# Graph layer with gathered and sorted edge groups: seven sorted pairs at every eleventh group in place of ten at every eighth

## Chip, cores and metric

The kernel runs on one core of a Trainium2 chip. The metric is the device time of one launch in microseconds (us). The engines are named as the profile names them: PE (TensorE), PEld (its weight loads), DVE (VectorE), ACT (ScalarE), POOL (GpSimd) and SP (SyncE).

## What is computed

One layer of a graph network on 6250 nodes of 128 features, with 100,000 edges that are sorted by destination, each with four attributes:

```
msg_in = concat([x[src], x[dst], edge_attr])          # 100000 x 260
h = silu(msg_in @ mW1 + mb1)                          # 100000 x 128
aggregated = segment_sum(h @ mW2 + mb2, dst, 6250)
u = silu(concat([x, aggregated]) @ uW1 + ub1)
y = layer_norm(x + u @ uW2 + ub2, ln_g, ln_b)
out = layernorm(x + y)
```

The kernel multiplies the node features by the two halves of mW1 first (tables A for sources and B for destinations), so that an edge needs the sum of a row of A, a row of B and four attributes times a small matrix. It sums the silu values by destination with a one-hot product and applies mW2 to the sums.

## The kernel before, in words

**Groups.** The edges are cut into 98 groups of 1024 (8 tiles of 128; the last has fewer). A group's destinations lie in a window of at most 80 nodes. The groups are worked off in one of two ways.

A **listed** group gets its rows of A by indirect DMA: POOL issues one gather for each tile (`fetch`, L272, `ga<-tab_a,src_i`), eight for a group, four listed groups ahead (`AHEAD`), into six buffers. DVE makes a matrix st of destinations (L670) and a one-hot matrix oh (L680). PE forms B's rows and the attributes' part (`pre<-mv,st`, eight products of one kind, 16 matmul records), DVE adds the gathered rows to it (L722, two halves), ACT takes silu (L724, two halves), and PE sums by destination (`pt<-oh,h`). One listed group is one **stage** of the program's main loop (`for j, g in enumerate(listed)`), and the hidden values of a group are made in the stage before its sums.

A **sorted** group gets no gathers. Sorted groups come in pairs k, k + 1. At the start of the program the edges of these groups are sorted by source (a bitonic sort on DVE, four rows of it for each group). With sorted sources, the rows of A are selected on PE: one-hot matrices O are multiplied by A, which lies in the core's memory in three bf16 pieces (`po<-O,A` for two of them, `po<-O,A_low` for the third); a window of the edges is enough for each block of nodes. A pair is worked off in four **parts** of 512 edges. For each part SP loads sources and destinations (`load_part`, L1089 to L1095, `sc<-sd` and `ar<-sd`), DVE makes st_s (L1114) and Oc, ACT makes most of O (squares at L1138 and relu at L1139, `picks`), PE multiplies the attributes (`pn<-Oc,at_s`, `attribute_part`) and adds B's rows (`po<-st_s,mv_s`), then comes the selection (`select`), ACT takes silu of the finished part (hT, L1198), PE turns it (`pn<-ident,hT`, `turned_hidden`), ACT copies it (h_s, L1209), and PE sums by destination (`pn<-oh,h_s`).

**The order of the work** is written out by hand. `Q0`, `QD` and `QN` give the first sorted group, the distance from pair to pair and the number of sorted groups. `SPAN` is QD - 2: the selection of a pair is spread over the listed stages between it and the pair before. Each stage has two slots for selections, one ahead of its sums and one behind (`slot(j, 0)` and `slot(j, 1)`). `shares` says how much of a pair's four parts each slot takes. `load_at`, `match_at`, `pick_at`, `part_at` and `turn_at` say for each of the four parts how many stages ahead of the pair its loads, its DVE matrices, its one-hot matrices O, its attribute products and its turning come; `ROWS` and `ATTR` say the same for the pair's rows of B and its attributes.

The gathers are paced. Every second gather waits for a product of PE (`paced`, at the end of the loop): the one that PE has reached 3.5 stages (`PACE`) ahead of the gather's own, counted in PE's work between pairs:

```
t -= (PACE if g < NG - 2 else PACE - 1) + NEAR * max(0.0, 1 - (t - RAW - 1) / (2 * RAW))
...
until = begun[knots[k]] + share * (begun[knots[k + 1]] - begun[knots[k]])
```

The nodes are worked off in batches of 512 beside the groups: tables A and B before, and the layer's second half after the last group of a batch (`node_stage`: u, uT, y, z and o, with PE products into pn).

Of the kernel before, what the change touches and what calls it, by code (L numbers as in the profile page):

```python
# [27 lines left out]
def kernel(  # L28
# [54 lines left out]
    last = [G * k + G for k in range(NB - 2)] + [NG - 4, NG - 1]  # L83
    assert rest_t == 5 and last[NB - 3] == NG - 10

    Q0, QD, QN = 18, 8, 20
    firsts = [Q0 + QD * q for q in range(QN // 2)]
    by_sort = {k + u: 2 * q + u for q, k in enumerate(firsts) for u in range(2)}
    listed = [g for g in range(NG) if g not in by_sort]
# [7 lines left out]
    HB = GE // 2  # L97
    QB = GE // GR
    SPAN = QD - 2
    shares = (0.3, 0.3, 0.4, 0.25, 0.375, 0.375, 0.35, 0.3, 0.35, 0.35, 0.35, 0.3)  # L100
    assert len(shares) == 2 * SPAN and abs(sum(shares) - GR) < 1e-6
    load_at, match_at, pick_at = (9, 8, 6, 5), (8, 7, 5, 4), (8, 6, 5, 3)
    part_at, turn_at = (7, 6, 4, 3), (4, 3, 1, 0)
    ROWS, ATTR = 7, 8
    SLACK = 400.0
    LISTS = 4
    assert RS <= P and W <= S0 and S0 + G * ED == P and listed[RAW] == RAW
# [1551 lines left out]
```

## Time and profile before

| | us |
|---|---|
| median of three runs | 1002.12 (1001.17 to 1003.69) |
| the profiled execution | 1000.51 |
| its span, from first to last instruction | 998.6 |
| PE busy | 781.4 |
| DVE busy | 609.6 |
| POOL busy | 590.1 |
| ACT busy | 456.7 |

The mean granted clock of PE was 0.910. In a row of a timeline the first number is the start in the span, the second the duration, and the square bracket holds the idle time of the engine before it and what ended that ("issue" is time in which it waited for nothing that the profile shows). In a row of the windows stand the stretch, its length, the busy time of each engine with its count of instructions, the granted clock, the share of the DMA engines and GB/s. In a row of waits stand the total, the number of times and the longest.

### The profile page before, as it was taken

Reading aid. Unit: us, or ns where it says so; the run is one execution under the profiler, and the core shown is the slowest. Engines: PE = TensorE matmul, PEld = TensorE weight load, DVE = VectorE, ACT = ScalarE, POOL = GpSimd, SP = SyncE. Lnnn points to the kernel's source line nnn. Section 1 sums busy time; section 2 is a strip of 40 time slices with the busy share of each in tenths; the row PEclk is TensorE's granted clock in tenths of the full one; section 3 lists DMA queues with packets and bytes.
Section 4 is the critical chain, followed back from the end, with each engine's and each line's share of the span. In section 5 each row is a group of like instructions: output and inputs, shape, how many; then the busy total and the mean of one; then the engine's idle time right before and its main releaser. Section 6 shows DMA issues by size and latency. Waiting matters only on the chain.

```text
span 998.6 us, 17635 instructions
## 1 busy us (share of the span) xinstructions
PE 781.4 (78%) x6000; PEld 680.4 (68%) x6000; DVE 609.6 (61%) x1631; ACT 456.7 (46%) x710; POOL 590.1 (59%) x633
## 2 busy tenths in 40 slices
PE   4547666787987998888887887988887987887844
PEld 3547665676776777777777766776676776776633
DVE  5457686875566566556566566576476475474562
ACT  4453021555356356356445545455455555542252
POOL 6666666566666656656666666666666666665630
PEclk8669887998999998999999999999899898997976
DMA  8554344533434434425334324334334334232220
GB/s 232 156 144 133 95 121 104 133 101 91 118 79 119 117 77 118 114 76 129 88 80 130 85 80 132 77 87 126 82 84 125 86 77 133 77 94 60 81 63 16
DMA packets 115619, 102.85 MB, mean 103 GB/s; under 512 B 24374, under 2 KB 95878, under 8 KB 115522
## 3 DMA queue, kind: packets, MB, share of 16 engines
q1 hardware_dynamic: 83430, 54.87, 19.3%
q0 software_dynamic: 19904, 40.80, 16.9%
q10 hardware_dynamic: 12188, 5.98, 2.1%
q8 instruction: 49, 0.80, 0.3%
q14 instruction: 48, 0.39, 0.1%
HBM read 87.26 MB, written 14.32 MB: 102 GB/s over the span
## 4 chain that ended last, share of the span: by engine, by line
PE 70%; issue 16%; DVE 5%; ACT 3%; DMA 2%; another core or an unknown queue 1%; SPq 1%; POOL 0%; DVEq 0%; ACTq 0%; POOLq 0%
PE po L167 24%; PE pre L167 15%; PE pt L167 14%; PE pn L167 13%; PE pn L170 2%; PE pre L170 1%; DVE keys L973 1%; DMA near<-near_d 1%; SPq L1074 1%; ACT A L528 0%; POOL ga L272 0%; DVE bn L792 0%; ACT xT L500 0%; DVE st L670 0%
## 5 line engine op out<-in xcount | busy, mean ns | idle before, releaser
L272 POOL DMA_INDIRECT ga<-tab_a,src_i x582 | 550.3, 946 | 350.6 <-issue 155.5
L167 PE MATMUL po<-O,A 128*128 128x314 bf16 (+54 forms) x1400 | 202.6, 251 | 18.2 <-issue 18.2
L167 PE MATMUL pre<-mv,st 128*128 128x128 f32 x1244 | 176.5, 288 | 33.4 <-issue 29.7
L167 PE MATMUL pt<-oh,h 128*128 128x104 f32 x1244 | 176.8, 293 | 30.6 <-issue 27.1
L167 PEld LDWEIGHTS pre<-mv,st 128*128 128x128 f32 x1244 | 161.2, 201 | 51.7 <-issue 46.9
L167 PEld LDWEIGHTS pt<-oh,h 128*128 128x128 f32 x1244 | 164.1, 208 | 38.9 <-issue 38.3
L167 PE MATMUL po<-O,A_low 128*128 128x314 bf16 (+54 forms) x700 | 161.0, 252 | 16.8 <-issue 16.7
L167 PEld LDWEIGHTS <-A 128*128 128x128 bf16 x1400 | 124.1, 102 | 43.1 <-issue 24.2
L724 ACT ACTIVATE h<-ga 128x512 f32<-128x512 f32 x146 | 86.2, 624 | 123.6 <-DVE ga L722 58.9
L722 DVE TENSOR_TENSOR ga<-ga,pre 128x512 f32<-128x512 f32 x146 | 94.5, 677 | 39.9 <-remote 10.5
L1198 ACT ACTIVATE hT<-po 128x512 f32<-128x512 f32 x40 | 23.9, 597 | 197.7 <-remote 96.9
L670 DVE TENSOR_SCALAR_CACHE_REDUCE st<-near,p_rows 80x1024 f32<-80x1024 f16 x78 | 98.7, 1265 | 13.1 <-issue 7.8
L1138 ACT ACTIVATE O<-sc,p_less 128x512 bf16<-128x512 f16 x160 | 105.5, 707 | 0.0
L779 DVE TENSOR_TENSOR acc<-acc,pt 128x80 f32 x78 | 18.5, 237 | 136.0 <-remote 46.8
L1139 ACT ACTIVATE O<-O,ones 128x1024 bf16<-128x1024 bf16 x80 | 91.8, 1148 | 2.6
L167 PEld LDWEIGHTS <-A_low 128*128 128x128 bf16 x700 | 69.6, 100 | 25.3 <-issue 16.8
L334 DVE TENSOR_TENSOR O<-sc,held 128x512 bf16<-128x512 f16 x160 | 57.4, 415 | 34.4 <-remote 26.9
L680 DVE TENSOR_TENSOR oh<-held,rel 128x640 f32<-128x640 f32 x78 | 63.5, 814 | 0.1
L1209 ACT COPY h_s<-pn 128x512 f32<-128x512 f32 x40 | 23.3, 581 | 83.4 <-remote 28.4
L167 PE MATMUL po<-st_s,mv_s 128*128 128x256 f32 x160 | 49.5, 438 | 8.3 <-ACT hT L1198 4.4
L272 POOL DMA_INDIRECT ga<-in_x_dram,src_i x40 | 38.1, 952 | 23.9 <-issue 11.0
L167 PE MATMUL pn<-Oc,at_s 128*128 128x256 f32 x160 | 45.2, 408 | 3.3 <-issue 1.8
(232 smaller groups left out, 905.0 us busy)
## 6 DMA issues: line engine op xcount, KB each, us to landing
near<-near_d SPq DMA_DIRECT2D x78, 160.0 KB
sc<-sd SPq DMA_DIRECT2D x80, 128.0 KB
ga<-tab_a,src_i POOLq DMA_INDIRECT x582
ar<-sd SPq DMA_DIRECT2D x40, 80.0 KB
mv<-tab_b SPq DMA_DIRECT2D x78, 40.0 KB
tab_b<-o SPq DMA_DIRECT2D x11, 256.0 KB
out_dram<-o ACTq DMA_DIRECT2D x11, 256.0 KB
x<-in_x_dram SPq DMA_DIRECT2D x10, 256.0 KB
```

Of the source, the lines that this page charges most:

```text
L167: counted(nc.tensor.matmul(to, *operands, **flags), to, share)
L170: counted(nc.tensor.transpose(to, *operands), to)
L272: ins = nc.gpsimd.indirect_dma_start(out=rows[g][:, i, :], out_offset=None, in_=x if g < RAW else tab_a[:, :], in_offset=bass.IndirectOffs ...
L334: nc.vector.tensor_tensor(cut(to), cut(of), few[:p, None, :].to_broadcast([p, n // FEW, FEW]), op=OP.is_equal)
L670: nc.vector.tensor_scalar(stbuf[turn_of(g) % NST][:W], near.pop(g), p_col[:W], 0.0, op0=OP.is_equal, op1=OP.add, accum_out=deg_col(g),)
L680: nc.vector.tensor_tensor(oh[g][:, :n, :W], w_row[:, None, :].to_broadcast([P, n, W]), rel[:, g, :n, None].to_broadcast([P, n, W]), op=OP. ...
L722: nc.vector.tensor_add(s[:, i], s[:, i], of)
L724: nc.scalar.activation(h[:, i], of, AF.Silu)
L1138: nc.scalar.activation(O[:, j], key, AF.Square, bias=p_less[:, r : r + 1])
L1139: nc.scalar.activation(O[:, 2:], O[:, 2:], AF.Relu, bias=ones[:, 0:1], scale=-1.0)
L1198: nc.scalar.activation(now["hT", u], now.pop(("po", u)), AF.Silu)
L1209: nc.scalar.copy(now["h"][:, :, 2 * u : 2 * u + 2, :].rearrange("p g i f -> p g (i f)"), px.rearrange("p (g i) f -> p g (i f)", g=2),)
```

## The change

Only numbers change, at three places of the head of the function:

```diff
-    Q0, QD, QN = 18, 8, 20
+    Q0, QD, QN = 21, 11, 14
...
-    shares = (0.3, 0.3, 0.4, 0.25, 0.375, 0.375, 0.35, 0.3, 0.35, 0.35, 0.35, 0.3)
+    shares = (0.2,) * 5 + (0.25,) * 4 + (0.2,) * 5 + (0.25,) * 4
...
-    load_at, match_at, pick_at = (9, 8, 6, 5), (8, 7, 5, 4), (8, 6, 5, 3)
-    part_at, turn_at = (7, 6, 4, 3), (4, 3, 1, 0)
-    ROWS, ATTR = 7, 8
+    load_at, match_at, pick_at = (12, 10, 8, 5), (11, 9, 7, 4), (11, 8, 6, 4)
+    part_at, turn_at = (10, 8, 6, 3), (6, 4, 2, 0)
+    ROWS, ATTR = 10, 11
```

The pairs now begin at groups 21, 32, 43, 54, 65, 76 and 87 in place of 18, 26 and so on to 90. There are 14 sorted groups in place of 20, and 84 listed groups, that is stages, in place of 78. `SPAN` becomes 9 in place of 6, so a pair's selection is spread over 18 slots in place of 12. Selections begin in stage 11 in both versions; they end in stage 70 before and in stage 73 now. Of SP's 688 instructions 659 are left.

On POOL the whole difference is this, at the start of the program and over its length (`pos_i` belongs to the sort, whose arrays have four rows for each sorted group; `ga` are the gathered rows):

```order
 L284 IOTA floor_i 1x96
 L287 IOTA ceil_i 1x112
-L291 IOTA pos_i 80x256
+L291 IOTA pos_i 56x256
 L272 DMA ga<-in_x_dram,src_i 128x128 x32
-L272 DMA ga<-tab_a,src_i 128x128 x582
+L272 DMA ga<-tab_a,src_i 128x128 x630
```

There are 48 gathers more, and the arrays of the sort are narrower.

On PE, before, at the head of the stage of a pair, where the last part of this pair is turned and the selection of the next pair's first part begins (a number behind a name is that of a buffer; `pre` is the next listed group's, `po` the bank of the selection):

```order
L167 MATMUL po<-O,A_low 128x2x72
L167 MATMUL pn<-w_87,xB 128x128 x4
L167 MATMUL pre<-mv_236,st_250 128x128 x8
L170 MATMUL pn<-ident,hT 128x128 x4
L167 MATMUL pn<-Oc,at_s_1370 128x256
L167 MATMUL pn<-Oc,at_s_1371 128x256
L167 MATMUL po<-st_s_1366,mv_s_1368 128x256
L167 MATMUL po<-st_s_1366,mv_s_1369 128x256
L167 LDWEIGHTS A
L167 MATMUL po<-O,A 128x2x51
```

Now, on PE at the head of the same stage:

```order
L167 MATMUL po<-O,A_low 128x2x72
L167 MATMUL pre<-mv_235,st_250 128x128 x8
L170 MATMUL pn<-ident,hT 128x128 x4
L167 MATMUL po<-st_s_1369,mv_s_1371 128x256
L167 MATMUL po<-st_s_1369,mv_s_1372 128x256
L167 LDWEIGHTS A
L167 MATMUL po<-O,A 128x2x51
```

The attribute products of the next pair's second part (`pn<-Oc,at_s`) no longer stand between the turning and the next selection; they come a stage later (8 stages ahead of their pair, with 9 stages between pairs).

On ACT, before, between the silu of a finished part (`hT`) and the copy of its turned values (`h_s`), in the middle of the program:

```order
L1198 ACTIVATE hT<-po 128x512
L724 ACTIVATE h_89<-ga 128x512 x2
L1138 ACTIVATE O<-sc,p_less 128x512 x2
L1139 ACTIVATE O<-O,ones 128x1024
L1138 ACTIVATE O<-sc,p_less 128x512 x2
L1139 ACTIVATE O<-O,ones 128x1024
L1209 COPY h_s<-pn 128x2x256
```

Now, on ACT between the two:

```order
L1198 ACTIVATE hT<-po 128x512
L724 ACTIVATE h_88<-ga 128x512 x2
L1209 COPY h_s<-pn 128x2x256
L724 ACTIVATE h_89<-ga 128x512 x2
L1138 ACTIVATE O<-sc,p_less 128x512 x2
L1139 ACTIVATE O<-O,ones 128x1024
```

The making of O has moved from between the silu and the copy to behind the copy.

## The prediction

> **What bounds the kernel now.** I read the page first, engine shares and chain, to see whether one engine is full.
>
> ```profile
> PE 781.4 (78%) x6000; PEld 680.4 (68%) x6000; DVE 609.6 (61%) x1631; ACT 456.7 (46%) x710; POOL 590.1 (59%) x633
> ...
> PE 70%; issue 16%; DVE 5%; ACT 3%; DMA 2%; another core or an unknown queue 1%; SPq 1%; POOL 0%; DVEq 0%; ACTq 0%; POOLq 0%
> PE po L167 24%; PE pre L167 15%; PE pt L167 14%; PE pn L167 13%; PE pn L170 2%; PE pre L170 1%; DVE keys L973 1%; DMA near<-near_d 1%; SPq L1074 1%; ACT A L528 0%; POOL ga L272 0%; DVE bn L792 0%; ACT xT L500 0%; DVE st L670 0%
> ...
> L272 POOL DMA_INDIRECT ga<-tab_a,src_i x582 | 550.3, 946 | 350.6 <-issue 155.5
> ```
>
> The chain runs through PE, its largest part the selections into po. POOL looks idle for 41%, but its busy time counts only the 946 ns of a gather, not what lies between two. The timeline of POOL shows that.
>
> ```profile
> 929.65 0.94 POOL L272 DMA_INDIRECT ga<-tab_a,src_i  x1 [1.86 <-issue]
> 930.90 0.94 POOL L272 DMA_INDIRECT ga<-tab_a,src_i  x1 [0.30 <-issue]
> ...
> 938.39 0.94 POOL L272 DMA_INDIRECT ga<-tab_a,src_i  x1 [0.30 <-issue]
> 943.17 0.94 POOL L272 DMA_INDIRECT ga<-tab_a,src_i  x1 [3.83 <-issue]
> ```
>
> Eight gathers start back to back from 929.65 to 938.39, so a gather costs POOL (938.39 - 929.65) / 7 = 1.249 us, and a listed group at least 8 x 1.249 = **9.99 us**. Between such runs it stops, here for 1.86 and 3.83 us.
>
> Next, how long a stage takes. Each listed group ends in one row of sums, so the rows of this kind in PE's timeline count the stages (the first listed group is stage 0).
>
> ```profile
> 193.03 1.93 PE L167 MATMUL pt<-oh,h 128*128 128x104 f32 x16
> ...
> 924.17 1.93 PE L167 MATMUL pt<-oh,h 128*128 128x104 f32 x16
> ...
> 984.06 1.56 PE L167 MATMUL pt<-oh,h 128*128 128x104 f32 x12 [0.42 <-DVE acc L779]
> ```
>
> These are stages 11, 71 and 77. Selections begin in stage 11 and end in stage 70, so 60 stages with selections took 924.17 - 193.03 = 731.1 us, 12.19 us each; six of them, with one pair, make a period of 73.1 us. The six stages after that took 10.0 us each, and 998.6 - 984.06 = 14.5 us follow. Three windows of about a period show what fills it.
>
> ```profile
> 489.00:562.00 73.00, 61.37 (x499) 54.02 (x499) 45.08 (x119) 36.95 (x56) 44.81 (x49) 0.95 0.37 97
> ...
> 635.00:708.00 73.00, 62.67 (x504) 52.45 (x503) 44.48 (x118) 38.16 (x57) 44.10 (x47) 0.98 0.36 95
> sum 219.00, PE 184.45 PEld 158.62 DVE 134.41 ACT 113.23 POOL 133.96; mean PE 61.48 PEld 52.87 DVE 44.80 ACT 37.74 POOL 44.65
> ```
>
> PE works 61.5 of 73 us. POOL's 48 gathers cost 48 x 1.249 = 60.0 us. Both are at 82 to 84%: neither is full, each waits for the other a little. POOL's waits say how: every second gather waits for a product of PE.
>
> ```profile
> POOL ga L272 <- issue: 166.6, 462, 5.2
> POOL ga L272 <- remote: 71.8, 48, 2.1
> POOL ga L272 <- PE po L167: 41.5, 33, 1.9
> ```
>
> That POOL follows PE, and is not merely slow, shows in the lead: the last gather of stage 37 started at 473.36, its sums at 508.6; the very last at 964.36, with its sums at 984.06, 19.7 us later. POOL can fall back by some 15 us before PE waits for rows.
>
> ```profile
> 473.36 0.95 POOL L272 DMA_INDIRECT ga<-tab_a,src_i  x1 [0.31 <-issue]
> ...
> 964.36 0.94 POOL L272 DMA_INDIRECT ga<-tab_a,src_i  x1 [0.30 <-issue]
> ```
>
> **The change part by part.** *Three pairs fewer.* Six groups go back from selection to gathers: 582 + 6 x 8 = 630 gathers. PE by tile, in the same three windows (po; Oc; hT; h_s; pre; oh, which holds h_s too; pn, which holds Oc, hT and h_s too):
>
> ```profile
> sum 219.00, PE 75.44; mean PE 25.15
> ...
> sum 219.00, PE 13.54; mean PE 4.51
> ...
> sum 219.00, PE 8.00; mean PE 2.67
> ...
> sum 219.00, PE 11.80; mean PE 3.94
> ...
> sum 219.00, PE 37.72; mean PE 12.57
> ...
> sum 219.00, PE 49.60; mean PE 16.53
> ...
> sum 219.00, PE 45.93; mean PE 15.31
> ```
>
> A pair costs PE 25.15 + 4.51 + 2.67 + 3.94 = 36.3 us; a listed group (12.57 + 16.53 - 3.94) / 6 = 4.19 us. So the change takes 3 x 36.3 - 6 x 4.19 = 84 us of work from PE and lays 48 x 1.249 = 60 us on POOL. What that is worth depends on which of the two ends last.
>
> *The new period* is nine stages and one pair. PE: 61.5 + 3 x 4.19 + 1.6 for three eighths more node work (15.31 - 4.51 - 2.67 - 3.94 = 4.2 us in a period) = 75.7 us, 8.4 us a stage. Its stalls are 73.1 - 61.5 = 11.6 us now; if they grow with the gathers (0.24 us each, 72 of them) they become 17.4 and the stage 10.3 us; if they keep their share of PE's work, 14.3 and 10.0 us. POOL: 72 x 1.249 = 89.9 us, 9.99 us a stage. So PE and POOL come out level and **POOL is late next**. I take 10.2 us, between the POOL floor and PE's upper value: PE has fewer stalls to give than before, as the gathers no longer wait for it.
>
> *The sum.* Stages 0 to 11 stay (193.0). Selections then run without a break from stage 11 to stage 73, so 63 stages (12 to 74) at 10.2 = 642.6. Nine stages without selection, 75 to 83, at the 10.0 of before = 90. The end is 14.5. Together 940.1, against a span of 998.6. The profiled run took 1000.51 as a whole, 1.9 more than its span, and the median of the runs is 1002.12; with the 1.9 the forecast is **942 us**. A stage of 11.13 us would give back exactly the old span: (998.6 - 297.5) / 63.
>
> *Eighteen smaller parts.* Each half-stage slot now holds 0.20 to 0.25 of a part in place of 0.25 to 0.40. The count of matmuls of a pair stays, so this costs nothing by itself; it spreads 25.15 us of po over nine stages, 2.8 us in each in place of 4.2. Less selection stands between a group's pre and its sums, and that was cover for DVE and ACT:
>
> ```profile
> L722 DVE TENSOR_TENSOR ga<-ga,pre 128x512 f32<-128x512 f32 x146 | 94.5, 677 | 39.9 <-remote 10.5
> ...
> L724 ACT ACTIVATE h<-ga 128x512 f32<-128x512 f32 x146 | 86.2, 624 | 123.6 <-DVE ga L722 58.9 <-issue 34.5 <-DMA ga<-tab_a,src_i 13.8
> L1138 ACT ACTIVATE O<-sc,p_less 128x512 bf16<-128x512 f16 x160 | 105.5, 707 | 0.0
> L1139 ACT ACTIVATE O<-O,ones 128x1024 bf16<-128x1024 bf16 x80 | 91.8, 1148 | 2.6
> L1198 ACT ACTIVATE hT<-po 128x512 f32<-128x512 f32 x40 | 23.9, 597 | 197.7 <-remote 96.9 <-PE pre L167 43.9 <-PE po L167 30.5
> L1209 ACT COPY h_s<-pn 128x512 f32<-128x512 f32 x40 | 23.3, 581 | 83.4 <-remote 28.4 <-PE po L167 22.7 <-PE pn L167 10.2
> ```
>
> The hidden values of a group are made a stage before its sums, so the add and the silu (2 x 677 + 2 x 624 ns) have a whole stage of about 10 us. I cost it at 0; without that cover it would be 2.6 us a stage.
>
> *Re-timed loads and matrices.* A part's DMAs on SP, its one-hot on ACT and its attribute products now come up to three stages further ahead of the pair. SP has 29 rows fewer in all. Between hT and h_s, ACT had two pairs of O squares (2 x (2 x 707 + 1148) = 5.1 us) and now often has one silu pair (1.25 us), so it stands at h_s waiting for PE's transposes; behind it stands the silu of the next listed group, which isn't due for a stage. Even if all of ACT's work grew with the listed groups, it would have 37.7 x 9 / 6 = 57 of 92 us, and DVE 44.8 x 9 / 6 = 67 of 92, so neither becomes the bound. What PE itself waits for hT is a row of its waits:
>
> ```profile
> PE po L167 <- ACT hT L1198: 4.4, 4, 2.0
> ```
>
> Cost 0; the upper end is a wait of 2.0 us, the longest of these, in each of 28 parts, 56 us; the lower end the 4.4 us that would go.
>
> *The start.* The sort works on 56 rows of partitions in place of 80, with as many instructions of the same length along a row, and two steps of node work change places. I put it at 0, and between -3 and +3 us.
>
> **The rivals.** *(a) The pace stays (slower).* POOL is gated at every second gather; in the stretch with selections it ran at 60.0 of 73.1 us, 82%, the rest being stops like those of 1.86 and 3.83 us. If the stops are a price of each run and not PE's slowness, the stage goes on taking 12.19 us, 63 of them 768, and the time is 297.5 + 768 + 1.9 = 1067 us. It decides from 1.39 us per gather (11.13 / 8). For it: a stop of 3.83 us follows just the run of eight, the longest. Against it: the wait is on PE's products by the program, PE will reach them sooner, and at 929.65 POOL went eight without a stop.
>
> *(b) The clock (same to slower).* PE's granted clock is lower where PE is less busy:
>
> ```profile
> 132.00:193.00 61.00, 43.34 (x278) 38.87 (x278) 49.65 (x134) 15.21 (x24) 36.68 (x40) 0.85 0.45 115
> ...
> 924.20:984.10 59.90, 40.21 (x243) 33.59 (x241) 31.15 (x94) 20.39 (x35) 23.63 (x25) 0.83 0.22 60
> ```
>
> It was 0.85 and 0.83 there, at 71 and 67% busy, against 0.95 to 0.98 at 84%. If the 10.2 us stage of a PE that is busy for 82% sank to 0.84, its 75.7 us would become 75.7 x 0.97 / 0.84 = 87.4, with 17.4 of stalls 104.8, 11.6 us a stage, 297.5 + 731 + 1.9 = 1030 us; half the fall gives 11.0 us and 992. Against it: 82% is far nearer to the 84% of the warm windows. The Trainium skill, "TensorE: Matmul & The Clock Gate", HAM oscillation, says that the clock is halved when PE idles for more than about 3.4 us and that a kernel whose products wait for DMA pays at every step; if each of the 63 stages held one such wait and 3.4 us at half rate behind it, 1.7 us would be lost in each, a stage would take 11.9 us and the run 1049 (an estimate from that page). The trace agrees that such waits are rare so far, the longest ones being:
>
> ```profile
> PE po L167 <- issue: 38.8, 62, 3.2
> PE pre L167 <- issue: 31.5, 43, 3.9
> ```
>
> *(c) The lead is spent (faster still).* If POOL runs without any stop from stage 11's end, its 550 gathers that are left then take 687 us; with 19.7 and 14.5 after the last this gives 193 + 687 + 34.2 + 1.9 = 916 us.
>
> *(d)* The change not doing what it says: the order of the instructions shows 630 gathers and 28 parts, so I leave this out.
>
> **How the numbers follow.** Forecast (stage 10.0 to 10.7, 928 to 974): 0.43. (c): 0.12. (b): 0.18, of it 0.05 faster, 0.05 same, 0.08 slower. (a): 0.27. So faster 0.60, same 0.05, slower 0.35, where 0.3% is about what a measurement of this kernel can tell. The range reaches from (c), 916, up to 1050: it leaves out half of (a) and half of (c). Where the forecast holds, its own range is 928 to 974.
>
> **What would show it.** Right: stages of about 10.2 us between stages 11 and 74; POOL's gathers at 1.25 to 1.3 us each in runs much longer than four, with 39 in 50 us in place of 33; PE at 74 to 77% of the span; the chain with POOL or gathers in it. Wrong: as many stops as before and 33 gathers in 50 us (a); a granted clock under 0.9 in the middle (b); a lead that has fallen under 20 us by the middle (c). If hT or st_s stand ahead of long waits of PE, the smaller cover was the cause, which I cost at nothing.

## The result and the profile after

The changed kernel takes 1061.32 us (median of 4 runs, 1059.25 to 1064.07) where the kernel before takes 1001.64 (1000.47 to 1003.69): the ratio is 1.0595, with a 95% interval of 1.0564 to 1.0626. It is slower by 60 us; the forecast was 942.

The page of the changed kernel, with the rows that answer to those of before (shares, granted clock by slice, chain, gathers, and PE's products of a listed group):

```profile
span 1060.1 us, 16188 instructions
...
PE 785.6 (74%) x5322; PEld 679.5 (64%) x5322; DVE 581.6 (55%) x1532; ACT 397.2 (37%) x626; POOL 635.9 (60%) x681
...
PEclk8769786888988897898888888988888888877876
...
PE 57%; issue 17%; DVE 10%; another core or an unknown queue 7%; ACT 5%; DMA 2%; DVEq 1%; POOL 1%; SPq 1%; ACTq 0%; POOLq 0%
...
L272 POOL DMA_INDIRECT ga<-tab_a,src_i x630 | 595.9, 946 | 366.5 <-issue 204.8
L167 PE MATMUL pre<-mv,st 128*128 128x128 f32 x1340 | 222.4, 321 | 43.0 <-issue 29.5
```

PE has far fewer products and is busy for 4 us more than before: one product pre takes 321 ns in place of 288, at a mean granted clock of 0.825 in place of 0.910. Everything else has less to do. Only POOL has more, and its idle time has hardly changed (366.5 us in place of 350.6).

The sums of stages 74 and 83 in PE's timeline, which stand for 924.17 and 984.06 of before (stage 11 ends at 191.8, within 1.3 us of before):

```profile
956.73 1.48 PE L167 MATMUL pt<-oh,h 128*128 128x104 f32 x12
...
1045.76 1.45 PE L167 MATMUL pt<-oh,h 128*128 128x104 f32 x11 [0.42 <-DVE acc L779]
```

The 63 stages took (956.7 - 191.8) / 63 = 12.14 us each. Before it was 12.19. By the costs of the prediction a stage has 18% less work for PE (8.4 us for 10.25), and it takes the same time, as rival (a) had it. The nine stages without selection took 9.9 us each and the end 14.3 us, as forecast. The windows show gathers at the pace of before:

```profile
300.00:350.00 50.00, 39.49 (x288) 34.30 (x287) 26.00 (x59) 18.41 (x28) 30.58 (x33) 0.86 0.34 92
700.00:750.00 50.00, 40.06 (x278) 35.57 (x277) 22.57 (x48) 14.95 (x25) 31.43 (x34) 0.83 0.35 95
950.00:1000.00 50.00, 37.70 (x241) 33.37 (x242) 26.48 (x66) 14.14 (x24) 32.73 (x35) 0.81 0.28 80
```

Still 33 to 35 gathers in 50 us, in the stretch with selections and in the one without. How this looks close up, on POOL and PE of the changed kernel at the same time:

```profile
851.49 0.94 POOL L272 DMA_INDIRECT ga<-tab_a,src_i  x1 [2.33 <-ACT h L724]
...
860.28 0.94 POOL L272 DMA_INDIRECT ga<-tab_a,src_i  x1 [0.30 <-issue]
863.76 0.94 POOL L272 DMA_INDIRECT ga<-tab_a,src_i  x1 [2.53 <-issue]
```

```profile
858.64 0.33 PE L167 MATMUL pt<-oh,h 128*128 128x104 f32 x1 [0.45 <-issue]
860.04 0.25 PE L167 MATMUL pt<-oh,h 128*128 128x104 f32 x1 [1.07 <-issue]
861.47 0.33 PE L167 MATMUL pt<-oh,h 128*128 128x104 f32 x1 [1.18 <-issue]
862.89 1.42 PE L167 MATMUL pt<-oh,h 128*128 128x104 f32 x6 [1.10 <-issue]
```

Late in a run of eight gathers PE issues one product in 1.4 us, products that take 0.25 to 0.33 us and wait for nothing that the profile shows; 1.7 us after the run's last gather has ended (861.2) it goes on at full pace, and 0.9 us after that so does POOL.

The kernel before itself takes 819 to 825 us in some of the jobs on the chip and 997 to 1005 us in others, the first measurement among them, so each run is compared with the kernel before of its own job, and I call the jobs quick and slow by that.

### The profile page after: what moved, and what is told of

The parts are those of the page before. It is cut to its first block, busy times and chain, and to the rows that moved or that the text cites. A ratio compares the mean times of both kernels' runs of the same rounds, so it can differ in the third digit from the quotient of the medians.

```text
span 1060.1 us, 16188 instructions
## 1 busy us (share of the span) xinstructions
PE 785.6 (74%) x5322; PEld 679.5 (64%) x5322; DVE 581.6 (55%) x1532; ACT 397.2 (37%) x626; POOL 635.9 (60%) x681
## 4 chain that ended last, share of the span: by engine, by line
PE 57%; issue 17%; DVE 10%; another core or an unknown queue 7%; ACT 5%; DMA 2%; DVEq 1%; POOL 1%; SPq 1%; ACTq 0%; POOLq 0%
PE pre L167 16%; PE po L167 15%; PE pt L167 12%; PE pn L167 11%; PE pn L170 2%; ACT O L1138 1%; DVE ga L722 1%; ACT O L1139 1%; DVE keys L973 1%; PE pre L170 1%; DVE oh L680 1%; DVE bn L792 1%; DVE st L670 1%; POOL ga L272 1%
## 5 line engine op out<-in xcount | busy, mean ns | idle before, releaser
L272 POOL DMA_INDIRECT ga<-tab_a,src_i x630 | 595.9, 946 | 366.5 <-issue 204.8
L167 PE MATMUL pre<-mv,st 128*128 128x128 f32 x1340 | 222.4, 321 | 43.0 <-issue 29.5
L167 PEld LDWEIGHTS pre<-mv,st 128*128 128x128 f32 x1340 | 204.8, 233 | 57.4 <-issue 41.9
L167 PE MATMUL po<-O,A 128*128 128x114 bf16 (+32 forms) x980 | 162.2, 267 | 25.9 <-issue 25.8
L167 PE MATMUL po<-O,A_low 128*128 128x114 bf16 (+32 forms) x490 | 122.3, 267 | 14.0 <-issue 14.0
L167 PEld LDWEIGHTS <-A 128*128 128x128 bf16 x980 | 94.4, 108 | 53.8 <-issue 37.6
L1138 ACT ACTIVATE O<-sc,p_less 128x512 bf16<-128x512 f16 x112 | 73.8, 706 | 0.0
L1139 ACT ACTIVATE O<-O,ones 128x1024 bf16<-128x1024 bf16 x56 | 64.3, 1148 | 1.8
L167 PEld LDWEIGHTS po<-st_s,mv_s 128*128 128x128 f32 x112 | 26.4, 262 | 51.4 <-ACT hT L1198 27.6
L334 DVE TENSOR_TENSOR O<-sc,held 128x512 bf16<-128x512 f16 x112 | 39.5, 414 | 0.2
```

What stands on the lines that cost most here:

```text
L167: counted(nc.tensor.matmul(to, *operands, **flags), to, share)
L272: ins = nc.gpsimd.indirect_dma_start(out=rows[g][:, i, :], out_offset=None, in_=x if g < RAW else tab_a[:, :], in_offset=bass.IndirectOffs ...
L334: nc.vector.tensor_tensor(cut(to), cut(of), few[:p, None, :].to_broadcast([p, n // FEW, FEW]), op=OP.is_equal)
L1138: nc.scalar.activation(O[:, j], key, AF.Square, bias=p_less[:, r : r + 1])
L1139: nc.scalar.activation(O[:, 2:], O[:, 2:], AF.Relu, bias=ones[:, 0:1], scale=-1.0)
```

## The experiments

Theories: **G**, POOL's gathers set the time, each costing a fixed time. **C**, PE sets it, slowed by its clock. **P**, the wait of every second gather for PE's products, seen late, sets it.

The first run without the pacing, the one with pre twice, the first without selection and the first with half of the gathers were priced from 1061 us and met quick jobs. Their times lie outside every range that was expected for them; they are read against 882.13 us, which the changed kernel took in another quick job.

**The pacing left out** (changed kernel).

```diff
-        tc.add_manual_dep(ins.ins, product_at[...].ins.name, ...)
+        pass
```

> The changed kernel without the pacing: gathers wait only for their buffers and queue. Theory P (the wait for PE's products, seen late, holds POOL at 1.48 us per gather): gathers then go at 1.25 us, runs far longer than eight, 39 in 50 us, the time falls to 930 to 980 us. Theory G (a gather costs POOL or its queue about 1.48 us with the stop behind its run, whoever waits): still 33 to 34 in 50 us, 1050 to 1070 us. Theory C (PE, slowed by its clock and by the gathers, sets the time): gathers go faster at first and then wait for buffers, the time stays within 2%, 1040 to 1080 us.

872.91 us, in a quick job (before 821.58). 662 gathers ran without one stop (never more than 0.32 us idle between two).

> The changed kernel without the pacing, once more. On a chip where before takes about 821 us: 870 to 876 us as before. On a chip where before takes about 1001 us: if the late wait on PE's products makes POOL's stops there (theory P), gathers at 1.25 us and 870 to 960 us; if the gathers stop by themselves (theory G with 1.48 us each), 1045 to 1065 us.

This one fell into a slow job (before 1005.12): 1261.52 us, a ratio of 1.257 (1.240 to 1.274), far outside of both expectations. The first 50 us of the two runs of this one kernel, quick job and slow job:

```profile
0.00:50.00 50.00, 28.04 (x183) 24.33 (x183) 31.44 (x87) 30.34 (x57) 36.22 (x47) 0.91 0.88 250
```

```profile
0.00:50.00 50.00, 8.59 (x45) 7.07 (x45) 11.55 (x40) 8.32 (x15) 35.98 (x47) 0.67 0.54 144
```

POOL does the same in both, 47 instructions, most of them gathers back to back. In the quick job PE has 183 matmuls beside them, in the slow one 45. After the last of the gathers from x POOL then stands still for 37 us:

```profile
53.83 0.94 POOL L272 DMA_INDIRECT ga<-in_x_dram,src_i  x1 [0.30 <-issue]
92.19 0.94 POOL L272 DMA_INDIRECT ga<-tab_a,src_i  x1 [37.41 <-DMA st<-ea_d]
...
POOL ga L272 <- ACT h L724: 315.7, 53, 16.9
```

The gather at 92.19 is the first from table A. The 40 gathers from x have filled five of the six buffers, so it can't be a buffer that it waits for; the last write of table A, which PE's products have to make first, starts at 89.5 us (47.4 in the quick job). Over the whole run POOL waits 315.7 us, 53 times, for the silu of a group whose buffer it needs. So in a slow job PE falls behind beside gathers back to back, and POOL then waits for what PE hasn't made or used. The pacing isn't what costs the time there; as I read it, it keeps the runs short. P falls.

**PE with more work** (changed kernel, every product pre issued twice).

```diff
+            if not raw:
+                matmul(to, st[:, i, :], mv[turn_of(g) % NM], start=True, stop=True)
             matmul(to, st[:, i, :], mv[turn_of(g) % NM], start=True, stop=not raw)
```

> The changed kernel with every product pre of a listed group issued twice, the second over the first: about 79 x 1.9 = 150 us more work for PE, nothing else. Theory G (gathers at 1.48 us each set the time): within 2% of 1061 us, PE's granted clock up from 0.825 to over 0.9. Theory C (PE sets the time): 1120 to 1210 us. Theory P: PE gets on more slowly, so the paced gathers do too: 1100 to 1210 us.

885.51 us in a quick job, 3 us from the 882.13 of the changed kernel, with PE busy for 791.5 us in place of 689.3 and a granted clock of 0.946 in place of 0.892. A hundred microseconds more on PE, and a warmer clock, move nothing. C falls for the quick jobs; in a slow job this kernel wasn't run.

**PE with less work** (changed kernel without the selection products).

```diff
-                        for a in parts_of(b):
+                        for a in ():
```

> The changed kernel without the selection products (po from O with A and A_low left out, 1470 matmuls); the one-hots are still made, gathers and pacing as they are. Theory G (gathers at 1.48 us each): the time stays at 1030 to 1065 us though PE has some 175 us less work. Theory C: falls by 100 us or more, to 890 to 960 us. Theory P: the pace runs with a lighter PE, 930 to 980 us.

883.89 us in a quick job: nothing again.

> The changed kernel without its selection products once more (1470 matmuls of po left out, one-hots still made). On a chip where before takes about 821 us: 880 to 886 us as in the run before. On a chip where before takes about 1003 us: if the stops of POOL add up to some 224 us whatever PE has to do (670 x 1.249 = 837, 1061 in all), 1040 to 1065 us; if the stops are the time in which PE catches up with its work between runs of gathers, 60 us or more below the changed kernel, under 1000 us.

1031.45 us in a slow job (before 996.77; ratio 1.0352, 1.0281 to 1.0423; the change has 1.0595 there). 1470 matmuls fewer give back 2.4% of before's time, 24 us, though PE is busy for 86 us less (699.3, for 785.6 in the first measurement). The time lies between the two ranges expected, so neither reading of the stops holds as it was put: PE's work counts a little there, not for what it takes.

**Both kernels as they are, in a quick job.**

> The kernel before, unchanged, for a profile on the chip of this call. Theory G (POOL's gathers set the time, 1.25 us each where nothing stops them, plus about 45 us ahead of the first of the long run and behind the last): on a chip that does it in about 821 us, 622 x 1.249 + 45 = 822, gathers without a stop; on a chip that does it in about 1001 us, stops as in the first profile.

> The changed kernel, unchanged. Theory G: 670 x 1.249 + 45 = 882 us on a chip where gathers run without stops, 60 us more than before, which is a ratio of 1.07; 1061 us on a chip with stops. Theory C (PE sets the time on any chip): not above before on the fast chip.

824.85 us (one run) and 882.13 us, as G had it from 622 and 670 gathers; against all runs of before in that job the ratio is 1.0769 (1.0701 to 1.0837). Windows of POOL of the changed kernel:

```profile
300.00:350.00 50.00, 37.81 (x41) 0.85 0.48 129
700.00:750.00 50.00, 37.81 (x41) 0.93 0.35 97
```

37.81 us of 50 in gathers is POOL without a stop: 40 gathers of 1.249 us.

**Gathers added to the kernel before.**

```diff
+        if g in again:      # 48 listed groups
+            nc.gpsimd.indirect_dma_start(out=rows[g][:, 0, :], out_offset=None, in_=tab_a[:, :],
+                in_offset=bass.IndirectOffsetOnAxis(ap=src_i[:, g, 0:1], axis=0))
```

> The kernel before with its ten pairs and its order, and 48 gathers more: in 48 listed groups tile 0 is gathered a second time to its own place. PE, DVE and ACT do what they did. Theory G (a gather costs POOL 1.249 us and gathers set the time): 48 x 1.249 = 60 us more than before, the very difference of the change (about 881 us where before takes 821, about 1061 where it takes 1001). Theory C (PE and its clock made the change slower): no more than 10 us over before.

871.51 us, +50 us where G had 60; ratio 1.0625 (1.0592 to 1.0657). The stops account for the missing 10: what the starts of two gathers lie apart beyond 1.249 us adds up to 16 us in the kernel before in a quick job, and to 4 us here. The 48 gathers, which aren't paced, seem to fill stops that were there.

> The kernel before with 48 of its gathers issued twice, once more. On a chip where before takes about 821 us: 868 to 873 us. On a chip where before takes about 1003 us: if each gather only adds its 1.249 us, 1061 to 1065 us; if a gather also holds PE up and PE sets the time, 1070 to 1090 us.

1058.69 us in a slow job (before 996.77), +62 us; ratio 1.0625 (1.0575 to 1.0675), against 1.0595 (1.0564 to 1.0626) of the change itself. The 48 gathers alone, with all ten pairs and before's order, make a loss as large as that of the change.

**Gathers taken from the changed kernel.** In 12 listed groups the second half is neither gathered nor added.

```diff
-        for i in range(tiles_of(g)):
+        for i in range(G // 2 if g in few_rows else tiles_of(g)):
...
-            if s is not None:
+            if s is not None and not (g in few_rows and k == 1):
```

> The changed kernel with 48 gathers fewer: in 12 of its listed groups, spread evenly, the second half is neither gathered nor added (its silu reads the product alone), so it has the 622 gathers of before. PE as in the changed kernel. Theory G: 60 us less than the changed kernel, back within 2% of before. Theory C or the re-timed parts at fault: within 10 us of the changed kernel.

831.78 us in a quick job: 50 us below the changed kernel of another quick job, where G had 60, and still 1.3% over before (1.0102 to 1.0162). POOL's stops have grown from 14 to 24 us here, which accounts for the rest.

**Seven pairs with before's distances and times** (`Q0, QD, QN = 18, 8, 14`).

> The kernel before with its distance of eight, its shares and its times of parts, and seven pairs in place of ten (the last at group 66): the number of gathers of the change without its re-timing. Theory G: as slow as the changed kernel, 60 us over before, within 1.5%. If the re-timing costs or gains something by itself, it shows as the difference from the changed kernel.

877.07 us; ratio 1.0685 (1.0642 to 1.0729), beside 1.0769 (1.0701 to 1.0837) of the change in another quick job. The intervals overlap, so the eighteen parts and the new times of loads and matrices can't be told from nothing.

**Half of the gathers.** The second half of every listed group is neither gathered nor added, `range(tiles_of(g) if g < RAW else G // 2)`, in the changed kernel first:

> The changed kernel without the gathers of the second half of each listed group, and without the DVE add of that half (its silu reads the product alone): 316 gathers in place of 630, PE as before. Theory G (gathers set the time): falls by up to 314 x 1.48 = 465 us until the next bound, PE's work of some 700 us at full clock: 780 to 880 us. Theory C with the gathers as what slows PE: also falls, 850 to 950 us, with the granted clock up. If PE's own waits set the time without the gathers: over 1000 us.

769.18 us, in a quick job; and once more:

> The changed kernel with half of its gathers once more (the second half of each listed group neither gathered nor added): 316 gathers from the table, PE's work as in the changed kernel. In a call where before takes about 821 us: 766 to 772 us. In a call where before takes about 1000 us: if the gathers are what makes the difference between the calls (they hold PE up, and PE holds them up), most of it goes with half of them, 770 to 860 us; if PE is slower there by itself, 900 us or more.

769.16 us, a quick job again. And in the kernel before:

> The kernel before with half of its gathers (the second half of each listed group neither gathered nor added): 292 gathers from the table in place of 582, ten pairs of selection as they are. It shows the bound behind the gathers. With seven pairs and half of the gathers the time was 769 us, PE busy for 85%; three pairs more are 84 us of PE work more. In a call where before takes about 821 us: if PE is the next bound, 790 to 815 us, hardly below the 821, so that still fewer gathers at the price of more pairs would gain next to nothing; if not, 750 to 775 us. In a call where before takes about 1000 us: under 860 us if the gathers cause the difference between the calls, over 900 us if PE is held up without them.

830.31 us in a slow job, where before takes 1003.59. Two windows of it:

```profile
200.00:250.00 50.00, 48.44 (x428) 43.52 (x428) 32.63 (x79) 30.33 (x48) 19.57 (x22) 1.00 0.38 100
700.00:750.00 50.00, 49.25 (x441) 44.05 (x439) 33.88 (x92) 30.13 (x47) 21.84 (x23) 1.00 0.37 88
```

PE is busy for 97 and 98.5% of them, at full clock. With half of the gathers, and these wide apart, PE isn't held up in a slow job: the hold-up comes with the gathers, and in these windows PE's own work is the bound. The kernel before with half of its gathers wasn't run in a quick job.

**Towards a faster version.** Eleven pairs at every seventh group (`Q0, QD, QN = 18, 7, 22`, ten shares of 0.4, times set anew):

> Eleven pairs at every seventh group, the numbers re-timed for that: 16 gathers fewer than before, PE with 36 us of selection more and 8 us of listed work less. Theory G: 16 x 1.249 = 20 us less than before on a chip without stops, as long as PE keeps below the POOL floor of 802 us. Theory C: up to 28 us more than before.

942.85 us in a quick job, 15% slower: POOL waits for PE, and PE for hT (28.3 and 17.0 us), Oc (27.3) and deg_s (13.9). My times for the parts were bad; it says nothing on the number of pairs. The kernel before without the pacing:

> The kernel before without the pacing. Theory G: 622 gathers without a stop, within 2% of before on a chip without stops (810 to 825 us). On a chip with stops: if the pacing makes them, 820 to 880 us; if gathers have them anyway, 990 to 1010 us.

> The kernel before without the pacing once more, timed in three rounds. On a chip where before takes about 821 us: 622 gathers without a stop, 805 to 815 us, 1 to 2% faster than before. On a chip where before takes about 1001 us: if the wait on PE's products, seen late there, makes the stops (theory P), gathers at 1.25 us and 810 to 880 us; if gathers there stop by themselves every few (theory G with 1.48 us each), 985 to 1010 us.

809.70 and 812.80 us, both in quick jobs; the second is 0.8% faster than before (0.9902 to 0.9941), the first 1.3% with a wider interval (0.9796 to 0.9938). It wasn't run in a slow job, and what leaving the pacing out of the changed kernel cost there makes it no version to keep.

## Why the prediction was wrong

Take 1.249 us for each gather (N of them, the 40 from x too) from each time; what is left is all that gathers back to back don't explain. The last column is the part of it in which POOL stops: the sum, over the run's trace, of what the starts of two gathers lie apart beyond 1.249 us. Start and tail make up most of the difference.

| kernel | N | job | us | us - 1.249 N | POOL's stops |
|---|---|---|---|---|---|
| before | 622 | slow, first measurement | 1001.6 | 225 | 185 |
| changed | 670 | slow, first measurement | 1061.3 | 225 | 188 |
| before, 48 more | 670 | slow | 1058.7 | 222 | 183 |
| changed, no selection | 670 | slow | 1031.5 | 195 | 160 |
| changed, unpaced | 670 | slow | 1261.5 | 425 | 356 |
| before | 622 | quick | 821.0 | 44 | 16 |
| changed | 670 | quick | 882.1 | 45 | 14 |
| changed, pre twice | 670 | quick | 885.5 | 49 | 16 |
| before, 48 more | 670 | quick | 871.5 | 35 | 4 |
| changed, unpaced | 670 | quick | 872.9 | 36 | 4 |

*What bounds the kernel.* Wrong, and the step that failed. I read 82% on POOL as slack: its stops, 2.2 us a stage (12.19 - 9.99), were to shrink to 0.2 (10.2 - 9.99) behind a lighter PE. They stayed at 2.15 (12.14 - 9.99). In a quick job both kernels run POOL nearly without a stop: there POOL is the bound. In a slow job, the kind of the forecast, the stops add up to 185 us before and 188 now, and 183 with 48 gathers added to before; they hardly follow PE's work. In both kinds 48 gathers added to before cost about what the change costs: 50 of 61 us, and 62 of 60.

That POOL itself is the bound isn't shown for slow jobs. There POOL waits for PE, and PE doesn't wait for rows: the last gather of stage 35 ends 40.0 us ahead of the stage's sums in the changed kernel, 35.5 before. The sum in the table describes these times, and the runs without selection and without pacing show that the rest is no constant.

*"PE has fewer stalls to give".* This is the term that was mis-sized. The forecast shrank a stage from 12.19 to 10.2 us, since the gathers would be allowed sooner; it measured 12.14. For nine stages and a pair it had 75.7 us of work on PE and 14.3 to 17.4 of stalls. In five windows of such a period (109.3 us each, from 300 us on) PE is busy for 85.3 us and idle for 24.0. PE's share of the span, 74%, lies in the range that I had named as a sign of being right; that is luck. Both terms came out larger; the 0.24 us of PE's stalls that I gave each gather (72 of them) would be 0.33, and the work on PE takes 9.6 us more beside them. In a slow job, as I read it, the stop behind a run is PE held up by the run, not PE's lack of speed, so a lighter PE shortens it little: 24 us for 1470 matmuls.

*The evidence was in the trace of before.* I quoted a row under rival (b) for its clock: 40 gathers in 61.0 us, PE busy for 71%, no selections. That is 1.53 us for a gather, as in the 73.1 us period with selections (48 gathers, 1.52). A pace that PE's work sets would have been quicker where PE had less to do. I read the rate of the follower in one stretch only.

*The work on PE.* Right in kind: a pair less is worth tens of us of PE. With half of the gathers PE is busy for 721.4 us with ten pairs (slow job) and 651.5 with seven (quick job), 70 us for my 84. With all gathers, in one quick job, it is 723.5 and 689.3, at granted clocks of 0.939 and 0.892. In the first measurement it was 781.4 and 785.6: there the lighter load is not to be seen in the time that PE is busy.

*The back-to-back time of a gather,* 1.249 us, was right, and 48 of them, 60 us, are the size of the result. That is partly luck in a slow job, where the same 60 us need the stops to stay at 185 us.

*Rival (a)* was right in its time, 1067 against 1061, and had 0.27. Its mechanism, stops that a lighter PE hardly shortens, fits slow jobs (a quick job has next to none); how PE is held up stays open.

*Rival (b).* The clock fell as it feared, 0.910 to 0.825, and its 87.4 us of work in a period are near the 85.3 measured. The Trainium skill, "TensorE: Matmul & The Clock Gate", HAM oscillation, has the clock sink where PE idles for long enough, and the traces agree in the direction: PE is busy for 78% before and 74% now. But the clock doesn't set the time: in a quick job it is 0.946 with pre twice and the time doesn't move, and in a slow job it is 0.764 without selections and the run is 24 us shorter. The rows that I quoted there as PE's longest waits were not the longest: the kernel before has single waits of 9.3 us for src_n and 7.1 us for xT.

*Rival (c)* and the parts costed at nothing: the lead wasn't spent in the first measurement (40.0 us at stage 35, given above). One sign that I had named did come. PE's wait for hT, 4.4 us before, costed at 0:

```profile
PE po L167 <- ACT hT L1198: 26.6, 5, 8.0
```

It isn't the cause of the loss, which comes with before's order too: with 48 gathers more (1.0625 in a slow job, 10.6 us of this wait) and with seven pairs at eight (1.0685 in a quick one). What shares, loads and times of parts cost in all can't be told from 0, while my own eleven pairs show that such times can cost over 100 us when they are set badly.

What stays open: what sets a slow job apart, by what way a gather holds PE up there, and whether POOL's own time or PE's is the one that 48 gathers lengthen. The gathers themselves last 945 to 946 ns in both kinds. The chip that the record numbers 15 had a quick job and a slow one, so the chip alone doesn't seem to set it.

## What to carry to other kernels

When two engines are both at about 80%, look at the rate of each in stretches where the other has little to do: one whose rate doesn't change, whatever it seems to wait for, is the first suspect, and its work must not be priced as free. Count an engine's cost with the gap between its instructions (1.249 us, not 946 ns), and test "N times that plus a rest" on the whole time before pricing any relief elsewhere. Adding the suspected cost to the old kernel (48 gathers, +50 and +62 us) shows in one run what it costs, though not by which engine.

## What the runs showed of the hardware

- In slow jobs PE issues one product in 0.7 or 1.4 us beside gathers back to back, with nothing in the profile to wait for, while DVE and ACT instructions keep their lengths (677 and 624 ns before, 678 and 626 after). Products that start 0.6 to 0.8 us after the one before: 78 before and 86 after in the first measurement, 121 unpaced; 17 and 12 in quick jobs; 12 with half of the gathers in a slow job. Those that start 1.3 to 1.5 us after: 27, 50 and 90; 2 and 6; 3.
- The same program on the same kind of chip took 821 or 1001 us by the job, with gathers of 945 and 946 ns in both.
- A gather (128 rows) takes POOL 1.249 us from start to start, 0.30 us of it between two; 662 ran so in a row.
